# A four-layer image kernel whose engine lists are ordered by the scheduler's other model of the machine

## The chip, the core and the metric

The kernel runs on one core of one Trainium2 chip. The metric is the device time of one execution in microseconds. Three executions of the kernel before took 9181.35, 9224.96 and 9217.53 us, with the median at 9217.53 us. Two measurements of one kernel are told apart here from about 0.5% on.

A core has five engines that matter below: PE (the matrix engine), DVE (vector), ACT (scalar), POOL (GpSimd, which here copies a little and issues the gathers) and SP (which issues nearly all other transfers). Each works through a list of instructions of its own, which was fixed when the program was built. Semaphores hold an instruction back until what it needs is there.

## The reference, cut to what matters

The input x has 16 images of 192 channels by 32 by 32, all fp32. Four residual layers are applied, each to a group norm of x:

```python
x = x + _L0_conv_ref(_gn(x), ...)   # mLSTM block + SiLU branch, 3x3 conv, batch norm over all images
x = x + _L1_conv_ref(_gn(x), ...)   # 6 heads: 6-qubit circuit makes q and k, softmax(-(|q-k|^2)/tau) @ v
x = x + _L2_conv_ref(_gn(x), ...)   # deformable depthwise 3x3: 9 taps, 4 corners each, at computed offsets
x = x + _L3_conv_ref(_gn(x), ...)   # 1x1 conv to 510, 2x2 FFT filter, depthwise 3x3, GELU gate, 1x1 conv
```

The batch norm of layer 0 needs all images, so the kernel has two phases.

## The kernel before

`circuits` makes the small circuit matrices. `phase_a` then does layer 0 for 32 half images (the recurrence in chunks of 128 tokens, and the 3x3 convolution by Winograd's method in one direction), and writes its result and the batch statistics to DRAM. `phase_b` does the rest for each of the 16 images in four streams of work:

- `vectors`: batch norm, group norm, the circuit's q and k.
- `attention`: for 48 pairs of heads (3 in each image), two passes over the scores. In `largest`, each of 16 steps has two matmuls into a PSUM tile `pmax` (L1149) and one DVE reduction of it, `mx` (L1151). In `values`, each of 16 steps has two matmuls `pscore` (L1188), an exponential `pexp` on ACT (L1191) and two matmuls `pav` (L1180). The passes of pair i+1 and pair i alternate.
- `layer2`: `layer2_offsets` makes the table, the offset convolution `poffc` (L1303), and from it (L1315 to L1336 on DVE) the indices and weights of an image. `layer2_gathers` then has 36 taps for each image (4 blocks of pixels, 9 taps). A tap has two gathers on POOL into buffers `gt` (L1357, a ring of 6), two scalings on ACT (L1361), six multiply-adds on DVE (L1387), one multiplication on DVE (L1389) and a matmul that adds it up in PSUM, `pdef` (L1393).
- `layer3`: matmuls `phad` (L1438), DVE work on planes (L1450 to L1470), the depthwise steps `dc` (L1489), GELU (L1510) and the output matmuls `pout` (L1524).

The PSUM tiles `pmax`, `pscore`, `pcirc`, `phad` and `paug` share one ring of two (`big`). So PE can be at most about one such tile ahead of the engine that reads it, DVE for `pmax`.

The streams are Python generators, and `weave` takes a piece from whichever has the least accumulated cost. That makes one program order:

```python
weave([(stream(0, vectors), 86.0), (attention(g), 205.8, 1.27), (layer2(g), 155.5, 2.49),
       (stream(3, layer3), 131.9, 3.78)])
```

The program order gives each instruction its priority, but it isn't yet the order in the engines' lists. When the `TileContext` closes, its scheduler plays the program through on a model of the machine, and puts next on each engine's list the first instruction by priority whose inputs are ready in that model. So the model's durations settle what stands ahead of what. In short, the weights of `weave` set how far an image has got in each stream, and the model sets the fine order. Once built, an engine's list isn't changed at run time.

## Time and profile before

| what | value |
|---|---|
| median of three executions | 9217.53 us |
| the profiled execution, its span | 9200.76 us, 9199.0 us |
| PE busy | 8010.2 us, 87% of the span |
| DVE busy | 6945.0 us, 75% |
| ACT busy | 4235.8 us, 46% |
| POOL busy | 1784.4 us, 19% |
| phase A, about 230 to 3150 us | PE 2752.2, DVE 2144.2 of 2920 us |
| phase B, 3500 to 8500 us | PE 4473.8, DVE 3886.3 of 5000 us |

Busy time is the time in which an engine has an instruction in work, in one profiled execution. The ends of matmuls are modelled in it, and a matmul that is followed by a wait looks longer than one that is followed by another. A group's row in the profile names its source line, engine, operation and tiles, then how often it occurs, its busy time, the mean of one, and what the engine waited for before it. The trace has as many instructions on each engine as the list has, in the list's order, so each entry of a list can be given its time.

### The profile page before, as it was taken

Reading aid. Unit: us, or ns where it says so; the run is one execution under the profiler, and the core shown is the slowest. Engines: PE = TensorE matmul, PEld = TensorE weight load, DVE = VectorE, ACT = ScalarE, POOL = GpSimd, SP = SyncE. Lnnn points to the kernel's source line nnn. Section 1 sums busy time; section 2 is a strip of 40 time slices with the busy share of each in tenths; the row PEclk is TensorE's granted clock in tenths of the full one; section 3 lists DMA queues with packets and bytes.
Section 4 is the critical chain, followed back from the end, with each engine's and each line's share of the span. In section 5 each row is a group of like instructions: output and inputs, shape, how many; then the busy total and the mean of one; then the engine's idle time right before and its main releaser. Section 6 shows DMA issues by size and latency. Waiting matters only on the chain. (4 is left out here: it accounts for less than half of the span.)

```text
span 9199.0 us, 91391 instructions
## 1 busy us (share of the span) xinstructions
PE 8010.2 (87%) x30512; PEld 3387.7 (37%) x30512; DVE 6945.0 (75%) x14313; ACT 4235.8 (46%) x7395; POOL 1784.4 (19%) x1680
## 2 busy tenths in 40 slices
PE   5999999999999969998998988988988898988853
PEld 2555555555555532232333323323333233323221
DVE  6777777777777744668788778788788788778888
ACT  3444444444444424444454454444545444444432
POOL 0101000101001100222222222222222223223342
PEclk9899999999999979998998998999998998999965
DMA  1111111111111120433443443433333334334352
GB/s 50 43 43 45 44 43 50 43 43 46 44 43 50 40 55 21 136 122 103 125 129 95 134 124 100 128 115 117 119 118 119 118 113 124 120 103 131 118 159 64
DMA packets 301028, 814.44 MB, mean 89 GB/s; under 512 B 47579, under 2 KB 164381, under 8 KB 300555
## 3 DMA queue, kind: packets, MB, share of 16 engines
q0 software_dynamic: 92160, 453.06, 15.8%
q1 hardware_dynamic: 208395, 355.55, 12.4%
q8 instruction: 239, 3.92, 0.2%
q14 instruction: 234, 1.92, 0.1%
HBM read 667.13 MB, written 132.94 MB: 87 GB/s over the span
## 5 line engine op out<-in xcount | busy, mean ns | idle before, releaser
L1357 POOL DMA_INDIRECT gt<-xg,ix x1152 | 1463.8, 1271 | 4235.7 <-DMA xn<-xnd 1165.5
L1387 DVE SCALAR_TENSOR_TENSOR acc<-gt,w,acc 128x192 f32<-128x192 f32 x3456 | 1213.0, 410 | 173.4 <-ACT acc L1361 147.5
L1151 DVE TENSOR_REDUCE mx<-pmax 128x2 f32<-128x1024 f32 x768 | 934.8, 1218 | 431.8 <-PE pmax L1149 429.5
L1149 PE MATMUL pmax<-kt,qt 64*128 64x512 f32 x3072 | 1097.0, 671 | 174.2 <-ACT pexp L1191 83.6
L1188 PE MATMUL pscore<-qt,kt 64*128 64x512 f32 x3072 | 1017.7, 690 | 196.7 <-DVE mx L1151 109.7
L1191 ACT ACTIVATE pexp<-pscore 128x1024 f32<-128x1024 f32 x768 | 780.5, 1017 | 739.2 <-PE pscore L1188 732.3
L1361 ACT ACTIVATE acc<-gt,w 128x192 f32<-128x192 f32 x1152 | 497.9, 451 | 1281.2 <-DMA gt<-xg,ix 1007.5
L1180 PE MATMUL pav<-pexp,vo 128*64 128x512 f32 x3072 | 962.4, 658 | 80.9 <-ACT pexp L1191 57.2
L508 POOL COPY qbd<-qT 32x384 f32<-32x384 f32 x512 | 303.9, 594 | 2847.6 <-PE se L542 2762.7
L1489 DVE SCALAR_TENSOR_TENSOR dc<-pad,wdw,dc 128x512 f32<-128x512 f32 x1152 | 807.1, 742 | 9.5 <-ACT dc L1487 9.1
L1393 PE MATMUL pdef<-acc,ident 128*128 128x384 f32 x1152 | 597.3, 604 | 125.4 <-DVE acc L1389 111.1
L538 ACT ACTIVATE dm<-dm,wtm 128x128 f32<-128x128 f32 x1536 | 490.6, 388 | 348.0 <-DVE dm L494 268.6
L1149 PEld LDWEIGHTS pmax<-kt,qt 64*128 64x128 f32 x3072 | 315.6, 197 | 757.8 <-issue 202.1
L1188 PEld LDWEIGHTS pscore<-qt,kt 64*128 64x128 f32 x3072 | 286.5, 201 | 712.2 <-issue 300.8
L550 PEld LDWEIGHTS pintra<-v,pt 128*128 128x128 f32 x3072 | 428.6, 213 | 164.1 <-issue 71.0
L550 PE MATMUL pintra<-v,pt 128*128 128x33 f32 x3072 | 437.7, 291 | 2.4 <-DVE pt L545 2.4
L1180 PEld LDWEIGHTS pav<-pexp,vo 128*64 128x64 f32 x3072 | 172.0, 141 | 662.9 <-issue 504.1
L1393 PEld LDWEIGHTS pdef<-acc,ident 128*128 128x128 f32 x1152 | 194.2, 210 | 563.2 <-DVE acc L1389 225.1
L545 DVE SCALAR_TENSOR_TENSOR pt<-se,dm 128x512 f32<-128x512 f32 x384 | 263.0, 685 | 144.5 <-PE se L542 143.5
L1049 PE MATMUL pz<-prob,amat 128*32 128x512 f32 x768 | 366.5, 603 | 0.9 <-ACT prob L1061 0.9
L1061 ACT ACTIVATE prob<-pcirc 128x1024 f32<-128x1024 f32 x192 | 195.6, 1020 | 351.3 <-PE pcirc L1059 344.8
L542 PE MATMUL se<-qbd,kT 64*128 64x256 f32 x1536 | 292.4, 450 | 54.1 <-DVE pt L545 54.1
(423 smaller groups left out, 12848.3 us busy)
## 6 DMA issues: line engine op xcount, KB each, us to landing
dm<-gd SPq DMA_DIRECT2D x128, 768.0 KB
xg<-xt SPq DMA_DIRECT2D x224, 192.0 KB
gt<-xg,ix POOLq DMA_INDIRECT x1152
xb<-x_in SPq DMA_DIRECT2D x32, 384.0 KB
y<-ydram SPq DMA_DIRECT2D x32, 384.0 KB
x1d<-xb SPq DMA_DIRECT2D x32, 384.0 KB
xnd<-y SPq DMA_DIRECT2D x32, 384.0 KB
xn<-xnd SPq DMA_DIRECT2D x48, 256.0 KB
```

The costliest lines, as they stand in the source:

```text
L538: nc.scalar.activation(dm[:, h, :], dm[:, h, :], AF.Exp, bias=wtm[:, c, 64 + h:65 + h])
L550: nc.tensor.matmul(pa[:, hh * 33:hh * 33 + 33], pt[:, h * 128:(h + 1) * 128], v33[:, hh, :], start=True, stop=True)
L1149: nc.tensor.matmul(pm[:, hh, :], qT[r, tt * 128:(tt + 1) * 128], kT[r, hf * HS:(hf + 1) * HS], start=True, stop=True)
L1151: nc.vector.tensor_reduce(mx[:, tt, hf, :], pm, AX.X, ALU.max, negate=True)
L1180: nc.tensor.matmul(po[0][hh * 64:hh * 64 + 64], vo[:, tt, hh * 32:hh * 32 + 64], pe[:, hh * HS:(hh + 1) * HS], start=(tt == 0), stop=(tt = ...
L1188: nc.tensor.matmul(ps[:, hh * HS:(hh + 1) * HS], kT[r, tt * 128:(tt + 1) * 128], qT[r, s], start=True, stop=True)
L1191: nc.scalar.activation(pe, ps, AF.Exp)
L1357: nc.gpsimd.indirect_dma_start(out=gt, out_offset=None, in_=xg, in_offset=bass.IndirectOffsetOnAxis(ap=ix[:, c:c + 1], axis=0))
L1361: nc.scalar.activation(acc[:, j, :], gt[:, 0:192], AF.Copy, scale=w4[:, 0, c:c + 1])
L1387: nc.vector.scalar_tensor_tensor(acc[:, j, :], gt[:, cr * 192:(cr + 1) * 192], w4[:, cr, c:c + 1], acc[:, j, :], ALU.mult, ALU.add)
L1393: nc.tensor.matmul(po[:, 0:384], cn.ident, acc.rearrange("p j c -> p (j c)"), start=(t == 0), stop=(t == 8))
L1489: nc.vector.scalar_tensor_tensor(out, src, w, add, ALU.mult, ALU.add)
```

## The change

The scheduler has two models of the machine that it can play the program on. The change asks for the other, which also times transfers and the queues that they wait in. Nothing is added, removed or resized by hand in the kernel's own code.

```diff
-    with tile.TileContext(nc) as tc:
+    with tile.TileContext(nc, schedule_with_timeline_sim=True) as tc:
         network(tc, d, out, nb)
```

Everything else follows from the order that the scheduler makes. Both programs hold the same 17024 matmuls, 14313 DVE, 7062 ACT, 1680 POOL and 1356 SP instructions. What the build adds around them differs: 316 loads of ACT's function tables in place of 333, 1948 stand-alone semaphore waits on DVE in place of 1474, and 411 on PE in place of 329. POOL's list is the same in both. On SP's, an entry stands 0.8 places from where it stood, on the mean, on ACT's 7, on PE's 11 and on DVE's 18. By line, the largest shifts are all in phase B: the matmuls `pdef` stand 51 places earlier on PE and L1387 20 places earlier on DVE, while `mx` stands 45 places later on DVE. In phase A the shifts are small (7 places on PE, 7 on DVE).

This is a piece of DVE's new list in phase B, with runs of equal entries put together:

```
L1387 acc x2, L1389 acc, L1151 mx, L32 gnmv, L1387 acc, L1389 acc, L1151 mx x5, L1220 att x2, L1151 mx x4,
L1450 pad x4, L1461 oe x2, ... L1489 dc x10, ...
```

## The prediction

> **What bounds the kernel now.** I read the page's head and busy times first, then the slices, then the stages of an image in phase B, then the waits.
>
> ```profile
> span 9199.0 us, 91391 instructions
> PE 8010.2 (87%) x30512; PEld 3387.7 (37%) x30512; DVE 6945.0 (75%) x14313; ACT 4235.8 (46%) x7395; POOL 1784.4 (19%) x1680
> PEclk9899999999999979998998998999998998999965
> ```
>
> PE has the most work and DVE comes next. Between them they leave little room, so the order in which they meet decides. Phase B repeats every 351 us for an image. The next lines are windows of two images, each cut where the 36 taps of layer 2 begin and end (us, then the busy time of PE, PEld, DVE, ACT and POOL with counts, PE's granted clock, DMA share, GB/s).
>
> ```profile
> 5116.00:5379.00 263.00, 223.86 (x768) 80.50 (x766) 226.09 (x467) 129.20 (x215) 80.98 (x66) 0.94 0.42 130
> 5379.00:5467.00 88.00, 86.43 (x336) 25.12 (x336) 56.50 (x101) 42.65 (x54) 7.02 (x7) 0.94 0.28 85
> 5467.00:5734.00 267.00, 227.05 (x764) 82.06 (x762) 225.91 (x467) 128.74 (x214) 84.54 (x65) 0.91 0.41 127
> 5734.00:5822.00 88.00, 86.26 (x335) 25.09 (x335) 56.53 (x100) 42.49 (x54) 7.03 (x7) 0.94 0.28 85
> ```
>
> There are two stages. In the tap stage PE and DVE are equally loaded, each at about 85%, and neither is full. In the gap between taps PE is full (86 of 88 us) and DVE is not. The mean of images 1 to 12 is 266.1 and 84.6 us, 350.7 together. DVE's waits in the first of these tap stages, and ACT's in the whole image, are:
>
> ```profile
> DVE mx L1151 <- PE pmax L1149: 11.6, 6, 6.4
> DVE pad L1450 <- ACT low L1445: 11.3, 3, 5.8
> DVE acc L1387 <- ACT acc L1361: 5.5, 5, 3.6
> DVE gngm L37 <- PE pgn L35: 3.5, 1, 3.5
> ```
> ```profile
> ACT acc L1361 <- DMA gt<-xg,ix: 63.5, 35, 6.3
> ```
>
> No wait of DVE dominates. ACT stands waiting for gathers half the time that it starts a tap (35 of 72), and can afford it. Last, the costliest DVE rows of the page, and a gather's timing in the timelines of POOL and ACT:
>
> ```profile
> L1387 DVE SCALAR_TENSOR_TENSOR acc<-gt,w,acc 128x192 f32<-128x192 f32 x3456 | 1213.0, 410 | 173.4 <-ACT acc L1361 147.5
> L1151 DVE TENSOR_REDUCE mx<-pmax 128x2 f32<-128x1024 f32 x768 | 934.8, 1218 | 431.8 <-PE pmax L1149 429.5
> ```
> ```profile
> 4610.26 1.12 POOL L1357 DMA_INDIRECT gt<-xg,ix  x1 [5.15 <-ACT pexp L1191]
> 4611.69 1.00 POOL L1357 DMA_INDIRECT gt<-xg,ix  x1 [0.31 <-issue]
> ```
> ```profile
> 4614.31 0.46 ACT L1361 ACTIVATE acc<-gt,w 128x192 f32<-128x192 f32 x1 [1.66 <-DVE dc L1489]
> 4616.31 0.46 ACT L1361 ACTIVATE acc<-gt,w 128x192 f32<-128x192 f32 x1 [1.54 <-DMA gt<-xg,ix]
> ```
>
> A gather takes 4 to 4.6 us from its issue to the instruction that uses it.
>
> **What the Trainium skill says.** "PSUM — Partial Sum Buffer", section "Engine vs sequencer instructions": the queues of ScalarE, VectorE and GpSimdE are strict FIFO, and matmuls start in program order. So an entry placed too early holds up all behind it; the trace agrees, with its instructions in the lists' order throughout. "Perfetto Trace Analysis", "Optimization Strategy": where the most-contended engine changes over time, interleaving the regimes may help. The windows above show two such regimes. "DMA: Bandwidth & Descriptors", "Anatomy of one DMA — SWDGE (gpsimd) path" gives 2.0 us plus bytes/436e3. For 128 rows of 3072 B that is an estimate of 2.9 us; the trace has 4 us and more, and I use the trace. "TensorE: Matmul & The Clock Gate", "What's actually happening": PE's clock falls when PE idles for some 3.4 us. The trace agrees in direction (granted 0.6 in the last slices, where PE is seldom busy).
>
> **The change, step by step.** No arithmetic is added or removed, so all the effect is in who stands before whom. I counted the entries of both lists between the same marks (first and last L1389 of an image on DVE, first and last L1393 on PE), and gave each entry the time that it takes up in the trace of before: its duration less its overlap with the next.
>
> 1. *Tap stage, DVE.* Before, image 6 has 459 entries between the marks: 208 L1387 (70 us), 34 `mx` (39), 52 L1489 (35), 35 L1389 (17) and others, 222 us. After, it has 407: 207 L1387, but 22 `mx` (25) and 40 L1489 (27), 185 us. Means of images 1 to 12: 222 before, 186 after.
> 2. *Tap stage, PE.* 430 entries and 226 us before, 304 and 161 us after.
> 3. *Gap.* DVE 60 before, 95 after. PE 87 before, 151 after. Part of PE's time in the tap stage is slow clock and modelled ends, which leave with the stall. With the median duration of each kind, PE's gap is 90 before and 140 after; before it really took 84.6. I take 142.
>
> So taps are bunched, and the balanced stage becomes one led by DVE (186 against PE's 161, or 142 by medians), followed by one led by PE. The maxima add up to 186 + 142 = 328, against 226 + 85 = 311 before. PE can't work ahead to use the slack, because `big` has two tiles and each `pmax` waits for a `mx` in DVE's list.
>
> 4. *Loss on top.* Before, the tap stage takes 44 us more than DVE's work. The 11.6 us of `mx` waits go, since PE will then be early. The waits on `low`, on ACT's scaling and on group statistics stay: 32 us.
> 5. *Gather ring.* In the trace a buffer's next gather is issued at the earliest 0.74 us after DVE's last read. Then come 4.1 us to ACT, 0.46 us there and 0.1 us to DVE, 5.4 us; and 1.3 us more for the second gather of the pair, about 7. The lists put this much other DVE work between a buffer's last read and its next first read: before, a median of 14.9 us, with 65 of some 1050 under 7; after, a median of 7.7 us, with 415 under 7. The shortfalls to 7 us add up to 470 us over all gathers, 235 over pairs, or 15 us for an image. Three taps are in flight and one stall serves the next two, so the lower end is a third of that, 5 us. I take 6.
> 6. *Sum.* Tap stage 186 + 32 + 6 = 224, gap 142, together 366 against 350.7: 15.5 us for each image, over about 14 images' worth (the first and last overlap less): +217 us. The break-even is a tap stage of 209 us.
> 7. *Rest.* The new list has 23 us less DVE work after the last `mx` (392 against 415), in a tail that DVE leads: −15. Dependent neighbours on DVE rise from 594 to 748; in the trace such a pair starts 0.115 us later than others: 18 us, half of it in DVE's stages, +8. The 17 table loads that go (1.28 us each, 22 us) are hidden by ACT's idle 54%. The 474 extra semaphore waits on DVE (0.02 us each) run under the preceding instruction. SP's entries move by less than one place; the mask rows `dm` of phase A have 5 us of slack and DVE wants them 3 us earlier. I cost these at nothing; without cover, 22 + 10 = 32 us.
> 8. *Phase A.* Cut at every second score step, max(PE, DVE) adds up to 3068 before and 3071 after: nothing, ±50.
>
> Total +210: 9217.5 + 210, about **9430 us** (the profiled execution, 9200.8, is 17 under the median, so there 9411).
>
> As a cross-check, independent of tap marks, I cut phase B at every 2nd, 4th, 8th and 16th `mx`, with its `pmax` on PE, and added up the larger of PE's and DVE's work. With the trace's own times the sums rise by 298, 256, 299 and 308 us; with medians for PE by 208, 187, 132 and 169. The sign doesn't depend on the cut.
>
> **The rivals.**
> - *The loss disappears with the balance* (faster): where one engine clearly leads, it rarely waits. If DVE's 44 us of idle in the tap stage fall to 9, tap 195 + gap 142 = 337, 14 less for an image, −190: 9030. Against it: in the last image's taps DVE also leads (151 of work, PE 73) and they took 179 us.
> - *No net effect*: the tap stage lands at its break-even of 209, within 3 us: 9217.
> - *The gather ring becomes the bound*: all 235 us of shortfall are added, in place of the 84 that I took (14 × 6), and stalls of DVE pass to PE through `big`: 9430 + 151, about 9580, and up to 9700 if PE's clock falls too. For it: ACT is already late half the time.
> - The change doing nothing can be excluded, since the lists differ.
>
> **How the numbers follow.** Forecast (stages split, 9290 to 9560) 0.68; ring bound 0.12; no net effect 0.08; loss disappears 0.12. So slower by over 0.5% 0.79 (the forecast's lower edge gives up 0.01), the same 0.09, faster 0.12. The range of 9220 to 9640 leaves out the faster case and the top of the ring case. Half a per cent is what a measurement tells from no change here.
>
> **What would show it.** In the profile after: a tap stage of some 210 to 230 us in which DVE is over 85% busy and PE at 75% or less; a gap of about 145 us with PE full; `pmax` and `pscore` waiting for `mx` much more than before; `mx` waiting for `pmax` only in the gap; ACT waiting longer for gathers; phase A unchanged. I am wrong if the tap stage comes out under 209 us, or if phase A or the tail moves by over 60 us.

## The result, and the profile after

The changed kernel takes 9776.8 us (median of 4 runs, 9759.8 to 9781.2) against 9207.3 (9181.4 to 9225.0, 4 runs): a ratio of 1.062 with a 95% interval of 1.059 to 1.065, or 570 us more. The forecast was 210 more, 9430 with a range to 9640. The direction was right. The size was not, and the mechanism of the forecast, a split of phase B's loads, is only a part of what happened.

The head of the page after the change, its busy times, and the granted clock by slices:

```profile
span 9779.4 us, 91859 instructions
PE 8057.6 (82%) x30512; PEld 3483.7 (36%) x30512; DVE 6979.8 (71%) x14313; ACT 4243.1 (43%) x7378; POOL 1935.3 (20%) x1680
PEclk9899899999998879998898897898888888988876
```

The work is nearly the same (PE +47 us, DVE +35) and the span is 580 us longer, so at this level the loss is idle time. That reading is too coarse, as the two phases show. The next lines are windows of the two phases, of before and then of after: phase A from the first to the last L545, phase B from the first to the last L1151. The columns are as in the prediction's windows.

```profile
174.80:3267.80 3093.00, 2917.59 (x12626) 1616.87 (x12626) 2266.92 (x4644) 1436.06 (x3059) 301.89 (x508) 0.94 0.13 44
3445.30:8690.40 5245.10, 4683.85 (x16658) 1582.86 (x16655) 4076.63 (x8105) 2549.10 (x3936) 1283.99 (x1044) 0.93 0.37 115
```

```profile
171.60:3429.40 3257.80, 3061.31 (x12635) 1679.22 (x12635) 2289.56 (x4652) 1451.76 (x3062) 302.86 (x509) 0.92 0.13 42
3596.30:9290.00 5693.70, 4606.39 (x16717) 1626.15 (x16715) 4113.42 (x8168) 2552.43 (x3937) 1460.30 (x1056) 0.87 0.35 107
```

Phase A is 165 us longer, and PE is *busy* 144 us longer in it, with the same instructions (first figure after the length). Phase B is 449 us longer although PE is busy 77 us less. The stretch between the phases is 11 us shorter, the tail 19, the start 3. The stages of two images in phase B, cut as before:

```profile
5403.00:5624.00 221.00, 172.22 (x569) 64.41 (x567) 186.95 (x412) 103.33 (x173) 87.63 (x66) 0.84 0.48 149
5624.00:5771.00 147.00, 128.92 (x530) 42.41 (x531) 95.79 (x156) 68.49 (x95) 7.67 (x7) 0.94 0.20 59
5771.00:6004.00 233.00, 173.99 (x542) 66.26 (x540) 188.63 (x415) 101.16 (x171) 96.48 (x65) 0.79 0.47 142
6004.00:6158.50 154.50, 136.47 (x558) 44.65 (x558) 94.70 (x152) 70.53 (x97) 6.74 (x8) 0.94 0.18 53
```

The mean over images 1 to 12 is a tap stage of 227.4 us and a gap of 150.7, together 378.1 against 350.7. DVE leads the tap stage (187 of 221 us in the first line) and PE does not fill the gap (129 of 147 us). Last, three DVE rows of the page; behind the second bar stands the idle time ahead of the group and what ended it.

```profile
L1387 DVE SCALAR_TENSOR_TENSOR acc<-gt,w,acc 128x192 f32<-128x192 f32 x3456 | 1268.4, 410 | 444.6 <-ACT acc L1361 407.8
L1151 DVE TENSOR_REDUCE mx<-pmax 128x2 f32<-128x1024 f32 x768 | 931.3, 1217 | 707.9 <-PE pmax L1149 707.1
L494 DVE TENSOR_TENSOR dm<-dm,causal 128x1536 f32<-128x1536 f32 x128 | 224.6, 1754 | 155.1 <-DMA dm<-gd 154.4
```

All three idle times have grown: 173 to 445 us ahead of the taps, 432 to 708 ahead of `mx`, 13 to 155 ahead of the mask's addition in phase A. These rows gave the first suspects. The runs showed that the last of them costs much less than its idle time.

### The profile page after: what moved, and what is told of

Its sections match the earlier page's. It is cut to its first block, busy times and chain, and to the rows that moved or that the text cites. A ratio compares the mean times of both kernels' runs of the same rounds, so it can differ in the third digit from the quotient of the medians.

```text
span 9779.4 us, 91859 instructions
## 1 busy us (share of the span) xinstructions
PE 8057.6 (82%) x30512; PEld 3483.7 (36%) x30512; DVE 6979.8 (71%) x14313; ACT 4243.1 (43%) x7378; POOL 1935.3 (20%) x1680
## 5 line engine op out<-in xcount | busy, mean ns | idle before, releaser
L1357 POOL DMA_INDIRECT gt<-xg,ix x1152 | 1611.0, 1398 | 4505.4 <-DVE w L1336 2587.6
L1387 DVE SCALAR_TENSOR_TENSOR acc<-gt,w,acc 128x192 f32<-128x192 f32 x3456 | 1268.4, 410 | 444.6 <-ACT acc L1361 407.8
L1151 DVE TENSOR_REDUCE mx<-pmax 128x2 f32<-128x1024 f32 x768 | 931.3, 1217 | 707.9 <-PE pmax L1149 707.1
L1149 PE MATMUL pmax<-kt,qt 64*128 64x512 f32 x3072 | 954.2, 711 | 357.1 <-ACT pexp L1191 162.6
L1188 PE MATMUL pscore<-qt,kt 64*128 64x512 f32 x3072 | 984.3, 711 | 243.9 <-ACT pexp L1191 86.0
L1180 PE MATMUL pav<-pexp,vo 128*64 128x512 f32 x3072 | 926.0, 676 | 69.6 <-ACT pexp L1191 69.4
L1393 PE MATMUL pdef<-acc,ident 128*128 128x384 f32 x1152 | 567.4, 602 | 196.7 <-DVE acc L1389 193.5
L538 ACT ACTIVATE dm<-dm,wtm 128x128 f32<-128x128 f32 x1536 | 469.3, 389 | 598.0 <-DVE dm L494 564.1
L1149 PEld LDWEIGHTS pmax<-kt,qt 64*128 64x128 f32 x3072 | 281.4, 208 | 908.9 <-DVE mx L1151 299.8
L542 PE MATMUL se<-qbd,kT 64*128 64x256 f32 x1536 | 364.3, 476 | 118.6 <-DVE pt L545 118.5
L1059 PE MATMUL pcirc<-psiT,lqk 64*128 64x512 f32 x768 | 227.8, 673 | 139.7 <-DVE mx L1151 104.3
L494 DVE TENSOR_TENSOR dm<-dm,causal 128x1536 f32<-128x1536 f32 x128 | 224.6, 1754 | 155.1 <-DMA dm<-gd 154.4
```

The lines of the kernel that those rows point to most:

```text
L538: nc.scalar.activation(dm[:, h, :], dm[:, h, :], AF.Exp, bias=wtm[:, c, 64 + h:65 + h])
L1149: nc.tensor.matmul(pm[:, hh, :], qT[r, tt * 128:(tt + 1) * 128], kT[r, hf * HS:(hf + 1) * HS], start=True, stop=True)
L1151: nc.vector.tensor_reduce(mx[:, tt, hf, :], pm, AX.X, ALU.max, negate=True)
L1180: nc.tensor.matmul(po[0][hh * 64:hh * 64 + 64], vo[:, tt, hh * 32:hh * 32 + 64], pe[:, hh * HS:(hh + 1) * HS], start=(tt == 0), stop=(tt = ...
L1188: nc.tensor.matmul(ps[:, hh * HS:(hh + 1) * HS], kT[r, tt * 128:(tt + 1) * 128], qT[r, s], start=True, stop=True)
L1357: nc.gpsimd.indirect_dma_start(out=gt, out_offset=None, in_=xg, in_offset=bass.IndirectOffsetOnAxis(ap=ix[:, c:c + 1], axis=0))
```

## The experiments

In all of them the kernel is the one of before, and each engine's list is fixed entry by entry, by dependencies that set the order alone and add no wait of their own. The base is either the old lists or the new ones; the diffs, cut to what matters, show what was changed beyond that. Where nothing was touched, the times of the changed kernel came back (phase A 3257.0 us in one run, phase B 5684.8 in another, 9783 in all with one PSUM bank changed).

### Phase A: the mask's transfer

The buffer `dm` has two tiles. After the change there are 2.3 us of DVE's work (median of the summed durations) between the last read of a tile and the addition L494 on its next contents, against 6.4 before. In the traces the round takes 4.05 us: 0.07 from the release to SP's issue, 3.6 to the landing, and the rest to the start.

```diff
 DVE's list, new; mask of chunk k
-  L494 dm(k)   L433 hc   L515 num   L486 cst   L398 kT
+  L433 hc   L515 num   L486 cst   L398 kT   L494 dm(k)
```

> All lists as the change makes them, but each addition of the mask to `dm` (L494) stands later in DVE's list, by a median of 5 entries, so that at least 4.6 us of DVE's work lie between the last read of the buffer (third L545 of the chunk two before) and it; in the changed list the median is 2.3 us. Theory 1 (the addition stands too close behind the release of its buffer, and DVE waits for the transfer): the 154 us of idle time ahead of L494 fall to some 15 and phase A from 3256 to about 3115 us, total about 9635. Rival (the new order of phase A is slower as a whole, and L494 is only where the lateness shows): the idle time turns up at the next entries, phase A stays over 3215, total over 9735.

Measured: 9894.9 us, 118 more than the changed kernel; phase A 3383. DVE's wait for the transfer is gone from the waits, but another has grown. ACT's waits for L494 in phase A (230 to 3150 us), after the change and then in this run:

```profile
ACT dm L538 <- DVE dm L494: 502.8, 106, 13.2
```

```profile
ACT dm L538 <- DVE dm L494: 875.3, 109, 24.5
```

The `dm` in these lines is the tile of the addition L494. The 12 exponentials of the chunk (L538) stand in ACT's list at their old place, ACT stands still until the later addition comes, and what is queued behind them on ACT is late for DVE in turn. Moving one entry on one engine passes the wait on. So the next run took the cause away and moved nothing. Its exponentials also take one head's bias for all 12, so the masks and biases of the other 11 heads are left out:

```diff
-  dm = p2.tile([128, 12, 128], ...)
-  nc.sync.dma_start(dm, gd[n, c])            # all heads, waits for dm's release
-  nc.vector.tensor_tensor(dm, dm, causal, ALU.add)
+  drow = p2.tile([128, 1, 128], ...)
+  nc.sync.dma_start(drow, gd[n, c, 0])       # one head
+  nc.vector.tensor_tensor(dm, drow spread over 12 heads, causal, ALU.add)
```

> All lists as the change makes them, but the mask's transfer goes to a small tile of its own (one head's 128 values, which the addition L494 then spreads over all 12 heads; the mask and the bias of the other 11 heads are left out). It no longer has to wait until the buffer of the chunk two before is released, and it is short; no entry moves. The run with a later addition took DVE's wait away and was still 118 us slower, because the 12 exponentials behind it then held ACT up. Theory 1a (the transfer behind the release makes the addition, and through it the exponentials on ACT, late): phase A falls from 3258 by 110 to 170 us, total 9610 to 9670. Rival (phase A is slower because its entries on ACT and DVE stand in a worse order, whatever the transfer does): phase A falls by less than 50, total over 9720.

> The lists of the kernel before with the same small tile for the mask (11 heads' masks and biases left out). A control: 13 us of DVE's idle time stand ahead of L494 there, so both theories expect 0 to 25 us less than before; if it gains over 60, the transfer was a bound before the change too and the change only shares it.

Measured: 9740.0 us with the new lists, phase A 3225, so 32 us less; 9209.8 with the old ones (ratio 1.000, 0.999 to 1.002). The rival of the run with the new lists holds: the transfer is not what makes phase A long. The idle time of 155 us ahead of L494 was real, but only 32 us of phase A hung on it.

One more run undid the change in phase A only:

```diff
 entries issued by 3435 us in the trace of after
-  new order
+  old order
```

> What the changed kernel had issued by 3435 us (phase A and the little of phase B that runs beside its end) in the old order, everything else in the new order. If the losses of the two phases are independent: phase A back to about 3091, phase B at about 5694 and a total of 9207 + 449 - 30 = about 9626. If the new order of phase A prepares phase B's, phase B differs by over 40 us from 5694, and the total lies outside 9580 to 9670.

Measured: 9601.0 us, phase A 3094.6 and phase B 5684.3. The two losses are independent, and so can be looked for one at a time.

### Phase A: halves that run at the same time

The waits did not show why PE was busy 144 us longer in phase A. PE's rows for three groups, one for each shape, before and after:

```profile
L542 PE MATMUL se<-qbd,kT 64*128 64x256 f32 x1536 | 292.4, 450 | 54.1 <-DVE pt L545 54.1
L266 PE MATMUL pz<-hn,wup 64*128 64x512 f32 x128 | 54.7, 638 | 0.0
L266 PE MATMUL plin<-x,wlin 64*128 64x512 f32 x128 | 36.1, 641 | 0.0
```

```profile
L542 PE MATMUL se<-qbd,kT 64*128 64x256 f32 x1536 | 364.3, 476 | 118.6 <-DVE pt L545 118.5
L266 PE MATMUL pz<-hn,wup 64*128 64x512 f32 x128 | 70.7, 641 | 0.0
L266 PE MATMUL plin<-x,wlin 64*128 64x512 f32 x128 | 71.8, 641 | 0.0
```

The mean of one (second figure behind the bar) hardly moves, while the busy time of the group doubles for `plin`. With 128 records of 641 ns, 36 us is less than half of their sum: they overlap. Such products use 64 of PE's rows, and two of them on different halves run side by side. The Trainium skill has this in "TensorEngine Tiling (Array Packing)", "Key Properties": tiles are independent and can run matmuls in parallel. The traces agree and add the price of order (medians): two halves of L542 that are neighbours in PE's list take 0.70 us from first start to last end, and 1.39 us of PE's time if other matmuls stand between them; for a pair of L266 it is 1.13 and 2.25. The new list has 68 of 384 pairs of L542 apart (3 before) and 78 of 96 pairs of L266 (32 before). One such place in PE's timeline after the change (start, duration, entry):

```profile
1272.01 0.70 PE L542 MATMUL se<-qbd,kT 64*128 64x256 f32 x2
1272.64 1.98 PE L396 MATMUL pk<-xa,wk 128*128 128x512 f32 x4
1274.46 1.10 PE L242 MATMUL pgn<-gnmv,g 128*128 128x1 f32 x7
1275.29 0.48 PE L542 MATMUL se<-qbd,kT 64*128 64x256 f32 x1
```

The first half runs alone at 1272.0, the second alone 3.3 us later. The run puts them back together:

```diff
 PE's list, new; 68 pairs of L542, 78 of L266
-  se(half 0)   pk   pk   pgn ...   se(half 1)
+  pk   pk   pgn ...   se(half 0)   se(half 1)
```

> All lists as the change makes them, but in PE's list two kinds of pairs of phase A stand side by side again: the two half-height products of a score step (`se`, L542), 68 of 384 pairs apart in the changed list and 3 in the old one, and the two of an up-projection (`pup`, `plin`, L266), 78 of 96 apart against 32. In the traces a pair of `se` takes 0.70 us side by side, since the two halves run at the same time, and 1.39 us of PE's time apart; the page has 72 us more for L542 and 36 more for L266 after the change. Theory 3 (phase A is longer because these pairs are apart, and PE, which is full there, pays for each half): PE's time falls by about 105 us and phase A by 70 to 130; total 9650 to 9710. Rival (PE's extra time is slack, the waits of ACT and DVE decide): phase A falls by less than 30, total over 9745.

Measured: 9663.7 us (ratio to before 1.050, 1.048 to 1.052), 113 less than the changed kernel. The profiled execution took 9634.2, 30 less than the median. Its window of phase A:

```profile
171.60:3309.80 3138.20, 2921.49 (x12635) 1652.44 (x12635) 2280.39 (x4652) 1435.87 (x3060) 298.77 (x508) 0.91 0.13 44
```

PE's work is back at the 2920 us of before and phase A is 120 us shorter, inside the 70 to 130 that theory 3 expected. So pairs apart cost phase A most of its loss, but the run doesn't undo the change exactly. It puts 146 pairs together, and 35 of them were apart before too: L266 takes PE 108 us here against 145 before and 196 after, L542 322 against 292 and 364. That leaves at least 45 of the 165 us. The mask's transfer was worth 32 by itself, and the two weren't run together.

### Phase B: the ring of gathers

The gathers' buffers `gt` form a ring: each is used again as soon as its last reader is done. The next runs give the ring two more buffers.

```diff
-  gt = p2.tile([128, 768], F32, tag="gt", name="gt", bufs=6)
+  gt = p2.tile([128, 768], F32, tag="gt", name="gt", bufs=8)
-  wdef = wp.tile([128, 9, 192], ...)     # used as wdef[:, t, :]
+  wdef = wp.tile([128, 1, 192], ...)     # used as wdef[:, 0, :], to make room
```

> All lists as the change makes them, with 8 buffers for the gathers in place of 6. To make room, one tap's depthwise weights are kept and used for all nine (the other eight taps' weights are left out; every instruction keeps its shape). With 8 buffers 21 gathers have under 7 us of DVE's work between release and next use, in place of 415. Ring theory: DVE's wait for ACT's scaling (25 us an image, 9 before the change) goes back to about 9, the tap stage falls from 227 to about 211 and the total by 16 x 16 = 260 to about 9520. Rival (the loss comes from the split into a DVE-led and a PE-led stage, and other waits take over when the ring is relaxed): at most 4 us an image, total over 9715.

> The lists of the kernel before, with 8 buffers for the gathers and one tap's weights for all nine, as in the run with the changed lists (eight taps' weights left out). A control: both theories expect 0 to 40 us less than before, since 65 of 1050 gathers were tight; 9170 to 9210. If it gains over 60, the ring was already a bound before the change.

> The lists of the kernel before, with 6 buffers for the gathers as before, and one tap's depthwise weights for all nine (eight taps' weights left out). A control for the two runs with 8 buffers, of which the one with the old lists gained 173 us where 0 to 40 were expected. If the buffers did that, this one stays within 20 us of before; if the smaller weights did it (a shorter load, another place in memory), it gains over 120.

Measured: new lists with 8 buffers 9549.2 us, 228 less; old lists with 8 buffers 9038.8 (ratio 0.982, 0.979 to 0.985), 173 less, where 0 to 40 were expected; old lists with 6 buffers and one weight 9210.7, so it is the buffers. The windows of phase B, with the new lists and then with the old ones, are:

```profile
3597.40:9079.90 5482.50, 4545.39 (x16717) 1604.95 (x16715) 4102.61 (x8168) 2533.49 (x3938) 1667.06 (x1058) 0.89 0.36 111
3428.70:8544.90 5116.20, 4652.98 (x16658) 1579.31 (x16655) 4072.41 (x8106) 2529.33 (x3936) 1414.07 (x1046) 0.93 0.38 118
```

In phase B the gains are 211 and 129 us. The ring cost time in both kernels, and the change made it dearer by the difference, 82 us.

How the old kernel could gain 129 us in phase B is seen in the waits of ten images. Before, with 6 buffers, and then with 8:

```profile
ACT acc L1361 <- DMA gt<-xg,ix: 616.4, 329, 6.4
DVE acc L1387 <- ACT acc L1361: 85.3, 65, 3.6
```

```profile
ACT acc L1361 <- DMA gt<-xg,ix: 132.5, 117, 2.4
DVE acc L1387 <- ACT acc L1361: 99.7, 76, 3.6
```

DVE waits for the taps no less than it did; it is ACT's own wait that has shrunk. ACT was busy 46% of the time, and still its standing at a gather had a price, since its other entries queue behind. The same ten images show where other waits shrank: DVE's for `pgn` (L37) from 50 to 6 us and for ACT's `low` (L1450) from 90 to 69, and PE's for `pexp` in `pmax`, `paug` and `pav` from 114 to 57. No run took these one at a time.

### Phase B: half way between the lists

> Every list half way between the two: each instruction is sorted by the mean of its start times in the traces of before and after. The work between the tap marks is then 201 us on PE and 205 on DVE, and 111 and 77 in the gap: the sum of the larger ones is 316 us an image against 313 before and 338 after. The gathers fall short of 7 us by 62 in all (20 before, 235 after), the additions of the mask short of 4.05 us by 90 (27 and 189). Theory of the split stages and the rings: phase B longer by 60 to 100 us, phase A by some 60, total about 9350 (9300 to 9390). Rival (every step away from the old order costs alike): half the loss, 9490.

Measured: 10916.4 us, far outside both. PE is busy 9536 us in it. In this order 1089 pairs of five kinds are apart (265 of `pmax`, 249 of `pscore`, 351 of `pav`, 74 of `pcirc`, 150 of `se`), so the run showed the pairs, not what it was made for. Its repair puts these together, and with them 194 pairs of two more kinds and the 92 fours of `poffc`:

```diff
 PE's list, half way
-  pmax(half 0)   pav ...   pmax(half 1)
+  pav ...   pmax(half 0)   pmax(half 1)
```

> The half-way lists, with the same halves side by side in PE's list: 265 pairs of `pmax`, 249 of `pscore`, 351 of `pav`, 74 of `pcirc`, 150 of `se`, 88 of `pup`/`plin`, 106 of `pconv`, and 92 groups of four of `poffc`. At 1.0 to 1.1 us for most, 0.7 for `se`, some 1150 us of PE's 9536 go. Theory 3 with the split stages (sum of the larger loads 316 us an image against 313): the 1700 us that the half-way lists lost come from pairs apart, and without it the total is 9300 to 9700. Rival (entries that depend on one another stand too close in a mixed order, on whatever engine): over 10200.

Measured: 9815.6 us; 1101 us came back. PE's busy time in the page (half way, then repaired) falls by more, 1457 us:

```profile
PE 9536.4 (87%) x30512; PEld 3730.2 (34%) x30512; DVE 6971.8 (64%) x14313; ACT 4295.3 (39%) x7445; POOL 1864.0 (17%) x1680
```

```profile
PE 8079.8 (82%) x30512; PEld 3378.2 (34%) x30512; DVE 6954.7 (71%) x14313; ACT 4288.5 (44%) x7445; POOL 1895.0 (19%) x1680
```

The total lies between the two theories. Why phase A is long in this mixed order (3570 us, PE busy 3131) was not followed up. Phase B alone tells more, next to the old lists with their pairs mended:

> The lists of the kernel before, with all halves that can run at the same time side by side in PE's list: 117 pairs of `pmax`, 22 of `pscore`, 82 of `pav`, 12 of `pcirc`, 46 of `pconv`, 32 of `pup`/`plin`, 3 of `se`. A pair of `pmax` takes 1.13 us together and 2.24 apart, one of `pav` 1.08 and 2.14: some 250 to 275 us of PE's time go. Theory 3: PE is at 86% and more, so half of it or more is gained, total 8950 to 9090. Rival (DVE is as loaded as PE in the tap stage, so the time only turns into waits): 9130 to 9210.

Measured: 9156.4 us (ratio 0.995, 0.993 to 0.996). Phase B fell by 94 us, phase A rose by 49 although PE's work in it fell by 28; why moving pairs of phase A hurts there was not found. In phase B the rival is nearer: of 257 us of PE's time that went, 94 were gained.

With these pairs together in all three but for a few, the means over images 1 to 12 are (us; PE's and DVE's busy time in brackets):

| lists | tap stage (PE, DVE) | gap (PE, DVE) | sum | phase B |
|---|---|---|---|---|
| old, pairs mended | 261.2 (215, 226) | 82.6 (78, 56) | 343.8 | 5151 |
| half way, pairs mended | 245.1 (197, 206) | 116.0 (104, 76) | 361.1 | 5417 |
| new, as they are (19 pairs and 44 fours of `poffc` apart) | 227.4 (170, 188) | 150.7 (133, 95) | 378.1 | 5694 |

The sum of the larger loads is 304, 309 and 321 us. It grows by 5 and then 12, while the time grows by 17 each step: 33 us more gap and 17 us less tap stage. So the larger loads do not by themselves explain phase B; what sets the length of the gap had to be found.

### Phase B: `mx` behind other work

In the gap of the changed kernel PE waits for `mx` entries that stand behind runs of `dc` in DVE's list, and a pair behind such a wait can take 2.08 us in place of 1.13. This one stands in the gap of the first stage shown above:

```profile
5679.27 2.08 PE L1059 MATMUL pcirc<-psiT,lqk 64*128 64x512 f32 x4 [5.56 <-DVE mx L1151]
```

```diff
 DVE's list, new; 375 of 768 mx
-  dc   dc   dc   dc   dc   mx
+  mx   dc   dc   dc   dc   dc
```

> All lists as the change makes them, but on DVE 375 of the 768 `mx` (L1151) stand earlier, by a median of 6 entries: each there where its `pmax` was ready in the trace of after. In that trace they start 1552 us later in all than their `pmax` ends (866 us in the trace of before), for they stand behind runs of independent `dc` (L1489), and PE, which has two `big` tiles, then idles: 1337 us in phase B against 808 before, 123 times over 3.4 us against 47; and of its pairs of 64-row products 362 took over 1.6 us in place of 1.1, against 187 before. Theory 4 (the late `mx` is the rest of phase B's loss): PE's gap goes from 150 to 130 to 140 us an image, the total to 9450 to 9650. Rival (the loads split between the stages are the loss, and DVE only works off the same entries in another order): gap over 146, total over 9720.

> The version that was faster than both kernels (old lists, pairs of phase B side by side, 7 buffers for the gathers, 2 for `pexp`; 9003 us), with 479 of the 768 `mx` earlier in DVE's list, by a median of 2 entries, each where its `pmax` was ready in the trace of before; 866 us of lateness in all. Theory 4: 8880 to 8970. Rival (in the balanced tap stage an earlier `mx` delays the taps by as much): 8985 or more.

Measured: 9781.5 us with the new lists, and a gap of 150.3. Over ten images PE's wait of `pcirc` for `mx` is gone (82 us before), and others came in its place: `pav` for `pexp` 141 us (47), `pdef` for the taps 137 (61); PE's waits sum to 776 us (746). With the best of the old lists (below) it was 9078.2, 75 us *more* than without. Theory 4 falls in both.

### Phase B: the chain that ends the gap

In every run up to here, but for the half-way lists with their pairs apart (129 us), the first tap of an image comes 87 to 95 us (means) after the last sum of its attention (L1227): group statistics, padding, transposes, the offsets' products L1303, their copy, four transposes L1310, positions, and the first gathers. Before, the attention ends 7 us ahead of the gap and the chain takes 91: the gap is 85 us. After, the attention ends 61 us into the gap and the chain takes 89: the gap is 151. So the chain is no longer than it was, and the gap grew because the attention ends later against the taps. But in the new lists the chain could be shorter. PE's timeline around its last step, before (the copy on ACT ends at 5807.0):

```profile
5805.22 1.07 PE L1303 MATMUL poffc<-xpad,woff 96*32 96x512 f32 x8
5806.21 1.08 PE L1180 MATMUL pav<-pexp,vo 128*64 128x512 f32 x4
5807.22 1.13 PE L1188 MATMUL pscore<-qt,kt 64*128 64x512 f32 x4
5808.28 0.66 PE L1310 MATMUL poff<-ident,ot 128*128 128x128 f32 x4
```

and after (the copy ends at 5737.9), with DVE's entry that waits for it:

```profile
5735.77 1.46 PE L1303 MATMUL poffc<-xpad,woff 96*32 96x512 f32 x8
...
5755.92 1.13 PE L1059 MATMUL pcirc<-psiT,lqk 64*128 64x512 f32 x4
5756.98 0.66 PE L1310 MATMUL poff<-ident,ot 128*128 128x128 f32 x4
```

```profile
5757.67 0.31 DVE L1315 TENSOR_TENSOR pos<-poff,gridb 128x144 f32<-128x144 f32 x1 [9.37 <-PE poff L1310]
```

Some 19 us of the next image's attention stand ahead of four transposes whose input is there. They can't simply move up, since `poff` takes over one of two PSUM tiles from `pmq`, which comes late in that attention; so it gets another bank.

```diff
-  pf = mm("poff")
+  pf = g.ps("pdef")
 PE's list, new
-  poffc   pmax   pscore   pav ... (19 us)   poff
+  poffc   pmax   pscore   poff   pscore   pav ...
 and L1315 to L1336 and the entries of the first taps, on their engines, up with it
```

> All lists as the change makes them, but the last part of the chain that leads to an image's first tap stands where its input was ready in the trace of after: the four transposes `poff` (L1310) on PE, 19 us earlier, the positions and weights on DVE (L1315 to L1336), and the entries of the first three taps with them, those of the next six by less and less. In the changed lists 19 us of the next image's `pmax`, `pscore`, `pav` stand before L1310 though its input was there, and DVE idles 9.4 us for it. So that PE needn't wait for the release of `pmq`, `poff` takes the free bank of `pdef`. Theory 5 (the gap lasts as long as the chain from the last sum of the attention to the first tap, and the new lists put other work into that chain): the gap falls from 151 to 130 to 138 us, and since PE has slack in the tap stage, most of it is gained: total 9500 to 9650. Rival (the loads of the stages set the time): what leaves the gap comes back in the tap stage, total over 9730.

> All lists as the change makes them, and only the bank changed: `poff` takes the bank of `pdef` in place of one of the two that `pz`, `pmq` and others share. A control for the run with the chain moved: both theories expect 0 to 30 us less than the changed kernel, 9745 to 9785.

Measured: 9704.2 us (ratio to before 1.053, 1.049 to 1.057) against 9783.1 for the bank alone, 79 less. PE's timeline in this run:

```profile
5711.79 1.46 PE L1303 MATMUL poffc<-xpad,woff 96*32 96x512 f32 x8
5713.17 1.13 PE L1149 MATMUL pmax<-kt,qt 64*128 64x512 f32 x4
5714.14 1.02 PE L1188 MATMUL pscore<-qt,kt 64*128 64x512 f32 x2
5715.09 0.66 PE L1310 MATMUL pdef<-ident,ot 128*128 128x128 f32 x4
```

A gap and the tap stage after it in this run are:

```profile
5599.90:5732.60 132.70, 114.08 (x479) 38.31 (x480) 94.96 (x155) 64.11 (x91) 7.79 (x8) 0.94 0.23 68
5732.60:5977.60 245.00, 194.00 (x594) 70.83 (x592) 190.20 (x416) 104.84 (x174) 87.55 (x64) 0.80 0.45 134
```

On the mean, the attention still ends 61 us into the gap, the chain takes 75 in place of 89, and the gap is 136.1 in place of 150.7, as theory 5 expected: the chain ends it. But the tap stage is 238.5 in place of 227.4, as the rival expected: three quarters of the gain come back there, where PE is now busy 186 us and DVE 189. Both are partly right, and the total lies between what the two expected. The place of this chain cost 65 us of phase B (74 against the control).

### Together, and a better kernel

> All lists as the change makes them, with the pairs of phase A side by side (as in the run that gained 113 us) and 8 buffers for the gathers with one tap's weights for all nine (the run that gained 228; eight taps' weights left out). If the two are independent causes in two phases: 9777 - 113 - 228 = 9436, 9415 to 9460, with phase A near 3138 and phase B near 5480. What then remains over the old lists with 8 buffers (9039) is the part that neither pairs nor ring explain. If they interact, the total differs by over 40 from that.

Measured: 9448.0 us (ratio 1.025, 1.023 to 1.027), phase A 3134.6 and phase B 5513.9. The two remedies add up to within 12 us, and the gain of the pairs in phase A is seen a second time. Against the old lists with 8 buffers, 409 us remain, 398 of them in phase B.

```diff
 old lists
+  halves of pmax, pscore, pav, pcirc side by side in PE's list
-  e4 = sb("e4", 3); gt ... bufs=6
+  e4 = sb("e4", 2); gt ... bufs=7
```

> A version meant to be faster than both: the lists of the kernel before, with only the pairs of phase B side by side (117 of `pmax`, 22 of `pscore`, 82 of `pav`, 12 of `pcirc`), since the run with all pairs had phase B 94 us shorter but phase A 49 us longer; and 7 buffers for the gathers, for which one of the three buffers of `pexp` is given up (in the trace of before the third is never needed: two would still leave 1.1 us). If the two gains add up: phase A 3093, phase B shorter by 94 for the pairs and by some 65 to 85 for the seventh buffer (the eighth and seventh together gave 129, and 24 in the tail), total 9020 to 9060. Rival (both gains use the same idle time): 9090 to 9120.

Measured: 9002.9 us (8998.8 to 9006.2), a ratio to before of 0.977 with an interval of 0.976 to 0.979. It leaves nothing out, and is faster than both kernels by 206 and 774 us. Phase A is 3089.5 and phase B 5060.5; the gains add up, and a little more than that.

## Why the prediction was right and wrong

Between the two profiled executions the time rose by 580 us, where 210 were forecast. Of the 370 us between, phase A is 165 (step 8) and phase B 232 (steps 3 to 6); the rest gives 27 back.

*Steps 1 and 2, work in the tap stage.* Right: forecast 186 on DVE and 161 on PE, measured 187.6 and 169.9. That slow clock would leave with the stall (step 3) did not come true: the granted clock in the tap stage fell from 0.90 to 0.81.

*Step 3, the gap.* "PE is full" there was wrong, and so the size: 142 forecast, 150.7 measured with PE busy 133. The gap ends when the chain to the first tap ends, 89 us after the attention's last sum, and that sum comes 61 us into the gap. Counting work between two marks can't see this. That the work came out near the chain's end is luck. Moving the chain up, past 19 us of other work, made the gap 136.

*Step 4, loss on top.* Forecast 32, and 6 for the ring; measured 227.4 - 187.6 = 39.8. The sum is right by luck. In the tap stages the waits of `mx` for `pmax` did not go; on the mean they fell from 15.4 to 10.4 us, and in the gaps they rose from 7.7 to 30.5. The waits for ACT's scaling, which were to stay but for the ring's 6 us, rose in the tap stages from 5.4 to 20.7. DVE's longest waits in the first tap stage shown after the change:

```profile
DVE acc L1387 <- ACT acc L1361: 14.2, 12, 3.0
DVE mx L1151 <- PE pmax L1149: 10.7, 5, 2.6
```


*Step 5, the gather ring.* Right for the difference: 5.0 us an image (378.1 - 363.9 for the new lists less 350.7 - 341.5 for the old) against 6. But the sentence on which it rests, that ACT waits for gathers "and can afford it", was wrong: two more buffers gave the old kernel 173 us. The ring rival's 9580 is nearer to the result than the forecast; its mechanism is not, since the ring's 82 us were in the forecast.

*Step 6, the sum.* Tap stage 224 forecast, 227.4 measured; with the gap, 366 against 378.1, so 27.4 us an image in place of 15.5 (15.3 by the rounded terms). And 449 us are 16.4 such images, not 14: the first and the last lose as much. Of the 27.4, the larger loads as measured (188 + 133 against 230 + 83) give 8.6, and idle time 18.8, of which 15.4 are in the gap.

*Step 7, the rest.* The tail went down by 19 (forecast 15). For `dm` the forecast took the slack of the old list, 5 us before use, and set against it that DVE wants it 3 us earlier. What counts is the time from the release of the buffer to its next use in the new list (2.3 us of work) against the round of 4.05 us. The idle time appeared as this says, 155 us, though it was worth only 32.

*Step 8, phase A.* This failed: nothing, ±50, was forecast, and 165 came. The loads were compared with durations from the trace of before, each "less its overlap with the next". For a half of a pair that overlap is with its other half, and it holds only while the two stay neighbours. In the new list 111 more pairs are apart; by the page that is 72 us for L542 and 51 for L266, and putting these pairs together, with 35 that were apart before too, took 120 us of phase A away. The same slip hid a gain in phase B: 117 pairs of `pmax` that were apart before stand together after, and `pmax`, `pscore` and `pav` cost PE 213 us less. In the old lists the same repair was worth 94 us of phase B, so the other losses there are larger than the 449 us show.

*The rivals.* "The loss disappears" and "no net effect" are excluded by the result. The condition "if phase A moves by over 60 us" is the one that applied.

*What stays open.* Of phase B's loss, the ring accounts for 82 us and the place of the chain for 65. They were not run together. Against the old lists as they are, some 300 of 449 us are left; against the old lists with their pairs together, which is the fairer base, some 400 of 543 (5151 to 5694). This rest grows evenly from the old lists over the half-way ones to the new, and an earlier `mx` does not cure it. That it is the price of the split is argued, not shown: the three lists differ in more than the split. The larger loads rise by 17 of the 34.3 us an image between the first and the last line of the table. No single wait carries the remainder: over ten images PE's waits sum to 746 us after and 375 before, and the ten largest kinds are 33 to 124 us each. The lower clock is a rival that no run tested: the granted clock fell from 0.90 to 0.81 in the tap stages and from 0.975 to 0.945 in the gaps (means of images 1 to 12). Whether that makes phase B longer or only follows from PE's waits is open.

## What to carry to other kernels

When an order changes, a duration from the old trace is only good for entries that keep their neighbours: look for matmuls on part of the array whose busy time is less than their count times their mean, and count how many pairs the new list parts. Then follow the chain that ends a stage, entry by entry, in the new lists; work between marks says what a stage needs at least, and an entry that stands ready behind 19 us of other work says what it will take. A wait is worth what a run without its cause gains: the 155 us ahead of the mask's addition were worth 32. And an engine that is half idle can still make others late when it stands at the head of its queue.

## What the runs showed that was not expected

- Two 64-row products next to each other in PE's list take 0.70 us (256 columns) or 1.13 us (512 columns) together; with other matmuls between them 1.39 and 2.25 (medians). Putting such products together gave the half-way lists 1101 us back.
- In one place, after PE had idled 5.6 us, the next pair of `pcirc` took 2.08 us in place of 1.13, and the `pmax` after it likewise.
- Two more tiles in the gather ring were worth 173 us of 9212 with the old lists, though DVE's wait for the taps did not shrink (8.5 us an image with 6 tiles, 10.0 with 8).
